# Cross-attention on one core: idle matrix products in TensorE's start, newer landing times in the plan, and other orders of the units of work

## The chip, the cores and the metric

The kernel runs on one core of one Trainium2 chip. The metric is the device time of one execution in microseconds (us): the median of 3 runs was 1946.18 us (1946.05 to 1948.58). Five engines work side by side, each through its own list of instructions in order: TensorE (PE, with its weight loads as PEld), VectorE (DVE), ScalarE (ACT), GpSimd (POOL) and SyncE (SP, which here only issues transfers).

## The reference

x and y (`ctx_2048`) are 32 x 256 x 1024, float32; the weights are 256 x 256.

```python
x_q = jnp.einsum('oc,bcn->bno', w_qk, y)
x_k = jnp.einsum('oc,bcn->bon', w_qk, x)
x_v = jnp.einsum('oc,bcn->bon', w_v, x) + b_v[None, :, None]
energy = jnp.einsum('bnc,bcm->bnm', x_q, x_k)
attention = jax.nn.softmax(energy, axis=-1)
attention = attention / (1e-07 + attention.sum(axis=1, keepdims=True))
x_r = jnp.einsum('bcn,bnm->bcm', x_v, attention)
x_r = jax.nn.relu(jnp.einsum('oc,bcn->bon', w_t, x - x_r) + b_t[None, :, None])
return x + x_r
```

## The kernel before

**The work.** Each of the 32 batches is a list of units. Every full-size number is split into three parts (tiles with a form index HIGH, LOW, REST), and each product is made as three products of parts, so one unit is 12 products of 128 x 512 on TensorE. The units of a batch, by the letters that the program uses:

- `k0`, `k1` (keys): x times the squared weight `gw`, into `gf`. ACT and DVE turn the sums into three forms.
- `v0`, `v1` or `V0`, `V1` (values): x times `vw`. DVE transposes the result into `turned`; SP writes `turned` to DRAM (`blocks`, four transfers) and reads it back in another layout (into `yr` or `turned`); ACT and POOL make the three forms `uf`.
- `W0`, `W1`: x times `tw`, which ACT copies to `xe` with a bias.
- `E0` to `E7` (energies): a 128 x 1024 tile of `energy`, from `gf` and the forms `yf` of y. DVE takes its minimum (`small<-banks`), ACT the exponential with a sum (`banks<-banks,small`), DVE the reciprocal; then for each half DVE adds to `acc`, ACT writes the HIGH form (`ef<-banks,small`), DVE the REST form (`ef<-banks,small,ef`), and last ACT and POOL the LOW form.
- `A0` to `A7`: `uf` times `ef`, summed over the eight tiles.
- `S`, `O`: sums of `acc`, and the end of a batch on DVE, POOL and ACT (`z`), with its stores.
- `X`, `Y2`, `Y3`: loading and splitting of the next x and y. y's forms are made with transfers that add, issued by POOL (`yf<-in_ctx_dram`, `yf<-yf`).

A batch has 22 units in the steady order: 8 E, 8 A, 2 k, 2 v, 2 W.

**Banks.** PSUM's eight banks are four pairs. The pairs of banks (4,5) and (6,7) hold the sums of the A units from A0 to A7, and outside that time other units, marked `^` in the orders; unmarked units take the pairs (0,1) and (2,3) in turn. A unit can start only when the pair that it takes has been read for the last time.

**What sets the order.** Five strings (`SET_UP`, `FIRST` for batch 0, `STEADY` for batches 1 to 29, `BEFORE` for batch 30, `LAST` for batch 31) give the order of the units on TensorE. The class `Plan` takes every instruction with an estimated duration, an estimated time from issue to landing, and what it reads and writes; it gives each a due time and sets the orders of the other engines from those. What it decides is then fixed: each engine takes its instructions in that order, so an instruction that waits holds up all behind it on its engine.

**Set-up.** `idle` products of the zero tile `few` (5 of them) come first on TensorE, then the square of w_qk (`G`, `banks<-z`), then the first keys (`f` with form, channel block and half), between them the transposes of w_t (`T`), the product of the bias (`b`) and the product of w_v and w_t (`Q`), all on raw x, w and y as they land.

**The end.** In the last batch `D1`, `G0` and `F1` finish the two halves of the channels: `F1` adds W1 straight into the sums of A, in pieces of 512, 256 and 256 columns.

All instructions carry line 231 of the profile, a helper that keeps each engine in order, so that they are told apart by their tiles.

Of the kernel before, what the change touches and what calls it, by code (L numbers as in the profile page):

```python
# [16 lines left out]
class Plan:  # L17
# [147 lines left out]


SET_UP = (
    "x0 x1 G fH00 fH10 fR10 fR00 T fH01 y fL01 fH11 b fR11 fR01 Q fL00 fL11 fL10"
)
FIRST = (  # L170
    "V0^ W1^ E0^ E1 V1^ W0^ E2 X E3 A0 A1 E4 E5 A2 A3 E6 E7 Y2 A4 A5 Y3 k1 v0 A6 A7 k0 S O"
)
STEADY = (
    "W0 E0^ E1 E2 V1^ W1^ E3 Y2 X A0 E4 A1 E5 A2 E6 A3 E7 A4 k1 A5 Y3 A6 v0 A7 S k0 O"
)
BEFORE = (
    "V1 E0^ E1 W0^ W1^ E2 A0 E3 E4 A1 A2 Y2 E5 E6 A3 E7 S A4 X Y3 A5 v0 A6 k1 k0 A7 O"
)
LAST = (
    "E0 R E1^ V1^ E2 E3 A0 A1 E4 A2 E5 A3 E6 E7 A4 A5 W0 A6 S a0 a1 D1 F1 G0"  # L180
)


# [1 line left out]
def kernel(  # L185
# [74 lines left out]
    def by_sync(landing, reads, writes, trace, early=0.0):  # L260
        plan.add("sync", 0.4, landing, reads, writes, trace, early=early)
# [13 lines left out]
    def accumulate(into, from_):  # L275
        pool.dma_start(into, from_, accum_op=ALU.add)
# [50 lines left out]
    def load_y(q):  # L327
        b, half = divmod(q, MH)
        s = q % NY
        f, r = yf[s], yr  # L330
        from_ = y[b].rearrange("(k p) n -> p k n", p=P)[:, :, ts(half, MB)]
        by_sync(7.0 if q else 7.8, [], ["yr"], lambda: sync.dma_start(r, from_))
        on_act(N, ["yr"], y_names(s, HIGH), lambda: act.copy(f[:, HIGH], r))

        def pieces(which):
            at = slice(which[0] * QB, (which[-1] + 1) * QB)
            high, low, third = (f[:, j, :, at] for j in range(FORMS))
            nh, nl, nr = (y_names(s, j, which) for j in range(FORMS))
# [12 lines left out]
            by_pool(8.0, nl + nr, nl, lambda: accumulate(value(low), value(third)))  # L351

        for which in ([0], [1]) if q == 0 else ([0, 1],):
            pieces(which)
# [4 lines left out]
    def load_x(b):  # L359
        for k in range(KC):  # L360

            def of(k=k):
                raw = [f"xr{k}{h}" for h in range(MH)]
                by_sync(6.0, [], raw, lambda: sync.dma_start(xr[:, k], x[b, ts(k, P)]))
                on_act(N, raw, x_names(HIGH, k), lambda: act.copy(xf[:, HIGH, k], xr[:, k]))
                on_pool(
                    N, raw + x_names(HIGH, k), x_names(REST, k),
# [4 lines left out]
                    lambda: act.mul(xf[:, LOW, k], value(xf[:, HIGH, k]), 1.0 / UP),  # L372
                )
                by_pool(
                    9.0, x_names(LOW, k) + x_names(REST, k), x_names(LOW, k),
                    lambda: accumulate(value(xf[:, LOW, k]), value(xf[:, REST, k])),
                )

# [41 lines left out]
    def values(b, q, j_pair):  # L420
# [151 lines left out]
    def finish(b):  # L572
        for c in range(KC):

            def of(c=c):
# [10 lines left out]
                by_sync(6.0, ["bias"], ["xo"], lambda: sync.dma_start(xo, x[b, ts(c, P)]))  # L586
# [5 lines left out]

            of()

    def ready_end(b):

        c = KC - 1
        raw = [f"xr{c}{h}" for h in range(MH)]
        on_act(
            N, raw + ["bias"], raw,  # L600
            lambda: act.activation(xr[:, c], xr[:, c], AF.Identity, bias=xbias[:, c], scale=1.0),
        )
# [35 lines left out]

            of()

    def end(b, c):

        p = pair(2 + c)
        for h in range(MH):
            cuts = [(0, MB)] if (c, h) != (KC - 1, MH - 1) else [(0, MB // 2), (MB // 2, MB)]
            for lo, hi in cuts:
                for j in ORDER:

# [197 lines left out]
    def set_up(token):  # L846
# [25 lines left out]
    def do(b, token):  # L872
# [15 lines left out]
        elif kind == "O":  # L888
            finish(b)
        elif kind == "R":  # L890
            ready_end(b)
        elif kind == "D":
            divided(n)
        elif kind == "G":
            beside(b, n)
        elif kind == "F":
            end(b, n)
        elif kind == "Y":
            if 2 * b + n < MH * B:
                load_y(2 * b + n)  # L900
# [45 lines left out]
```

## Time and profile before

| | |
|---|---|
| median of 3 runs | 1946.18 us (1946.05 to 1948.58) |
| the profiled execution, its own time | 1945.59 us |
| its span, first to last instruction | 1943.6 us |
| mean granted TensorE clock over the span | 0.998 |
| DMA, mean | 155 GB/s |

A time in the timeline is counted from the start of the span. A row gives start, duration (of a merged group: from its first start to its last end), engine, line, operation, tiles written and read, and count; in square brackets stands how long the engine sat idle before it, and what ended that. A row of the table by stage gives for each stretch the busy time of each engine with its count, the granted clock of TensorE (1.00 is full speed), the share of the DMA engines and GB/s.

### The profile page before, as it was taken

The page shows a single profiled execution, that of the slowest core. Times are in us where ns is not written, and L with a number is a line of the kernel's source. Part 1 is how long each engine was busy: PE and PEld are TensorE (multiplying, and loading weights), DVE is VectorE, ACT ScalarE, POOL GpSimd, SP SyncE. Part 2 cuts the span into 40 slices and gives each one's busy share as a digit, 9 for nine tenths or more (in the row PEclk, how much of TensorE's full clock was granted, in tenths as well). Part 3 has the DMA queues.
Part 4 walks back from the last instruction along what each step waited for, and adds up shares of the span by engine and source line. Part 5 has one row for each costly group of instructions (what it writes and reads, how often), then busy time and mean ns, then how long its engine had stood idle before and what let it go on. Part 6 is the DMA issues. An engine that isn't in the chain of part 4 may idle for free.

```text
span 1943.6 us, 24348 instructions
## 1 busy us (share of the span) xinstructions
PE 1930.7 (99%) x8492; PEld 1594.9 (82%) x8492; DVE 1496.1 (77%) x2107; ACT 1470.7 (76%) x1929; POOL 1554.5 (80%) x775
## 2 busy tenths in 40 slices
PE   9999999999999999999999999999999999999998
PEld 7788888888888888888888888888888888888877
DVE  6787777777777877778777777777787777877777
ACT  6679777797777887777977779777788777787665
POOL 5789777888777887778977788877888777897766
PEclk9999999999999999999999999999999999999999
DMA  6666765766666666666676576756666666667542
GB/s 178 142 155 166 178 151 132 163 167 177 155 141 148 163 174 174 141 149 157 164 181 149 132 163 167 179 155 139 151 163 174 171 142 147 158 165 182 141 98 76
DMA packets 128779, 301.75 MB, mean 155 GB/s; under 512 B 12944, under 2 KB 47248, under 8 KB 128656
## 3 DMA queue, kind: packets, MB, share of 16 engines
q1 hardware_dynamic: 92256, 200.19, 33.5%
q0 software_dynamic: 35680, 99.10, 29.7%
q8 instruction: 66, 1.08, 0.2%
q10 hardware_dynamic: 720, 0.92, 0.2%
q14 instruction: 57, 0.47, 0.1%
HBM read 167.25 MB, written 67.11 MB: 121 GB/s over the span
## 4 chain that ended last, share of the span: by engine, by line
PE 96%; DMA 1%; DVE 1%; ACT 0%; SPq 0%; POOL 0%; issue 0%; DVEq 0%
PE banks L231 96%; DMA blocks<-turned 1%; DMA yr<-blocks 1%; SPq L231 0%; POOL uf L231 0%; DVE ef L231 0%; DVE z L231 0%; DVE turned L231 0%; DVE acc L231 0%; DVE small L231 0%; POOL z L231 0%; ACT banks L231 0%; ACT uf L231 0%; ACT z L231 0%; ACT xe L231 0%
## 5 line engine op out<-in xcount | busy, mean ns | idle before, releaser
L231 PE MATMUL banks<-gf,yf 128*128 128x512 f32 x3072 | 730.2, 390 | 4.8 <-DVE ef L231 4.1
L231 POOL TENSOR_TENSOR ef<-ef 128x1024 fp32r<-128x1024 f32 x256 | 643.3, 2515 | 114.5 <-ACT ef L231 84.4
L231 PE MATMUL banks<-ef,uf 128*128 128x512 f32 x3072 | 731.7, 389 | 0.0
L231 PEld LDWEIGHTS banks<-gf,yf 128*128 128x128 f32 x3072 | 576.9, 188 | 127.6 <-DVE ef L231 6.6
L231 PEld LDWEIGHTS banks<-ef,uf 128*128 128x128 f32 x3072 | 577.0, 188 | 119.7
L231 DVE TENSOR_REDUCE small<-banks 128x1 f32<-128x1024 f32 x256 | 313.1, 1223 | 128.9 <-PE banks L231 126.6
L231 DVE SCALAR_TENSOR_TENSOR ef<-banks,small,ef 128x512 fp32r<-128x512 f32 x512 | 363.2, 741 | 21.6 <-ACT ef L231 21.4
L231 ACT ACTIVATE ef<-banks,small 128x512 fp32r<-128x512 f32 x512 | 333.9, 701 | 17.5 <-DVE acc L231 9.7
L231 ACT ACTIVATE gf<-banks 128x1024 fp32r<-128x1024 f32 x64 | 65.7, 1028 | 341.2 <-PE banks L231 341.0
L231 DVE SCALAR_TENSOR_TENSOR acc<-banks,small,acc 128x512 f32<-128x512 f32 x448 | 316.1, 746 | 6.8
L231 ACT ACTIVATE banks<-banks,small 128x1024 f32<-128x1024 f32 x256 | 280.6, 1096 | 38.4 <-DVE small L231 35.0
L231 ACT ACTIVATE ef<-ef 128x1024 fp32r<-128x1024 f32 x256 | 274.7, 1073 | 2.1
L231 POOL TENSOR_TENSOR z<-z,xe 128x1024 f32<-128x1024 f32 (+1 forms) x64 | 150.3, 2364 | 107.9 <-DVE z L231 105.4
L231 POOL TENSOR_TENSOR uf<-yr,uf 128x1024 fp32r<-128x1024 f32 x64 | 153.4, 2397 | 70.3 <-ACT uf L231 70.3
L231 PE MATMUL banks<-xf,gw 128*128 128x512 f32 x768 | 186.5, 392 | 1.9 <-ACT xf L231 1.9
L231 PE MATMUL banks<-xf,tw 128*128 128x512 f32 (+1 forms) x774 | 185.2, 388 | 1.6 <-DVE ef L231 0.7
L231 PE MATMUL banks<-xf,vw 128*128 128x512 f32 x768 | 184.6, 389 | 0.0
L231 POOL TENSOR_TENSOR uf<-turned,uf 128x1024 fp32r<-128x1024 f32 x64 | 167.6, 2619 | 5.7 <-DVE acc L231 3.3
L231 PEld LDWEIGHTS banks<-xf,tw 128*128 128x128 f32 x774 | 144.4, 188 | 32.8 <-DVE ef L231 1.7
L231 PEld LDWEIGHTS banks<-xf,gw 128*128 128x128 f32 x768 | 144.6, 189 | 32.5 <-ACT xf L231 2.3
L231 DVE RECIPROCAL small<-small 128x1 f32<-128x1 f32 x256 | 40.4, 158 | 168.5 <-ACT banks L231 168.5
L231 PEld LDWEIGHTS banks<-xf,vw 128*128 128x128 f32 x768 | 144.1, 188 | 30.2 <-DVE vw L231 0.3
(69 smaller groups left out, 1704.4 us busy)
## 6 DMA issues: line engine op xcount, KB each, us to landing
yr<-in_ctx_dram SPq DMA_DIRECT2D x64, 512.0 KB, 4.9
blocks<-turned SPq DMA_DIRECT2D x256, 128.0 KB, 2.9
yf<-in_ctx_dram POOLq DMA_DIRECT2D x63, 512.0 KB, 6.4
yf<-yf POOLq DMA_DIRECT2D x63, 512.0 KB, 4.7
xr<-in_x_dram SPq DMA_DIRECT2D x62, 512.0 KB, 4.2
xo<-in_x_dram SPq DMA_DIRECT2D x62, 512.0 KB, 4.5
xf<-xf POOLq DMA_DIRECT2D x62, 512.0 KB, 7.6
out_dram<-z SPq DMA_DIRECT2D x62, 512.0 KB, 4.9
```

The lines of the kernel that those rows point to most:

```text
L231: self.last = getattr(self.engine, name)(*args, **kwargs)
```

## The change

It does four things.

1. A token `z` in `SET_UP` issues one idle product of the zero tile `few` on TensorE. There is one before `G` and three behind it, beside the five that were there. The set-up's tokens also stand in another order: among others, the first key products are those of x's second channel block (`fH10`), and the load of y (`y`, which is enqueued on SP) stands behind `fH10`.
2. The estimated landing times in the plan are changed (y 7.0 to 5.8, x 6.0 to 5.0, the adding transfers 9.0 and 8.0 to 7.2 and 5.8, x's 9.0 to 8.2, `blocks` 2.4 to 3.0 and back 3.2 to 4.5, xo 6.0 to 5.2), and the estimated duration of the idle products and squares. These are inputs of the planner; no transfer is changed.
3. All five orders of the units are replaced. Of this table the diff shows two lines.
4. `R` takes its channel from the token and `end` is told whether it is the last; with the tokens `R1` and `F1` they issue what they issued before.

Apart from the four idle products no instruction is added or removed; the rest are moved.

```diff
 SET_UP = (
-    "x0 x1 G fH00 fH10 fR10 fR00 T fH01 y fL01 fH11 b fR11 fR01 Q fL00 fL11 fL10"
+    "x1 z G z z x0 z fH10 y fH00 fR10 T fH01 fL10 b fR01 fR00 fL01 Q fL00 fH11 fL11 fR11"
 )
...
 STEADY = (
-    "W0 E0^ E1 E2 V1^ W1^ E3 Y2 X A0 E4 A1 E5 A2 E6 A3 E7 A4 k1 A5 Y3 A6 v0 A7 S k0 O"
+    "W0^ E0^ E1 E2 W1^ V1^ E3 Y2 A0 E4 A1 E5 A2 X E6 A3 E7 Y3 S A4 A5 v0 k1 A6 A7 k0 O"
 )
...
-        by_sync(7.0 if q else 7.8, [], ["yr"], lambda: sync.dma_start(r, from_))
+        by_sync(5.8 if q else 7.8, [], ["yr"], lambda: sync.dma_start(r, from_))
...
-            by_pool(9.0, nr, nr, lambda: accumulate(third, from_[:, :, at]))
+            by_pool(7.2, nr, nr, lambda: accumulate(third, from_[:, :, at]))
...
-        plan.add("sync", 2.4, 2.4, ["turned"], ["blocks"], out_of)
+        plan.add("sync", 2.4, 3.0, ["turned"], ["blocks"], out_of)
         back, name = (turned, "turned") if q else (flat(yr), "yr")
-        by_sync(3.2, ["blocks"], [name], lambda: sync.dma_start(back, blocks))
+        by_sync(4.5, ["blocks"], [name], lambda: sync.dma_start(back, blocks))
...
-        plan.add("pe", count * (columns * 4 / 2400 - 0.08), 0.163, reads, writes, trace)
+        plan.add("pe", count * columns * 3.4 / 2400, 0.163, reads, writes, trace)
 
-    fp32_on_pe(
-        5, P, ["few"], ["bank7"],
-        lambda: [pe.matmul(banks[:, 7, :P], few, few, start=True, stop=True) for _ in range(5)],
-    )
+    def idle_products(count):
+        fp32_on_pe(
+            count, P, ["few"], ["bank7"],
+            lambda: [pe.matmul(banks[:, 7, :P], few, few, start=True, stop=True) for _ in range(count)],
+        )
+
+    idle_products(5)
...
+        elif token == "z":
+            idle_products(1)
```

**TensorE, the first rows of the program.** `few` is the tile of zeros, `z` holds the raw weights, `xf` the forms of x, `gw` those of the squared weight. Before:

```order
L231 MATMUL banks_95<-few_66 128x128 x5
L231 MATMUL banks_95<-z_90 128x256 x4
L231 MATMUL banks_95<-xf_74,gw_71 128x512 x8
L231 MATMUL banks_95<-z_90 128x128 x4
L231 MATMUL banks_95<-xf_74,gw_71 128x512 x6
```

The same place now:

```order
L231 MATMUL banks_95<-few_66 128x128 x6
L231 MATMUL banks_95<-z_90 128x256 x4
L231 MATMUL banks_95<-few_66 128x128 x3
L231 MATMUL banks_95<-xf_74,gw_71 128x512 x6
L231 MATMUL banks_95<-z_90 128x128 x4
```

One idle product stands ahead of the square and three between it and the first keys; the transposes come after 6 key products, where it was 8.

**TensorE, from A5 of batch 0 to the first energies of batch 1.** `uf1` and `ef` belong to the A units, `vw` to the values v0, `gw` to the keys k0 and k1, `tw` to W0, `yf0` to E0, E1 and E2. Before:

```order
L231 MATMUL banks_95<-ef1_81,uf1_77 128x512 x12
L231 MATMUL banks_95<-xf_74,gw_71 128x512 x12
L231 MATMUL banks_95<-xf_74,vw_72 128x512 x12
L231 MATMUL banks_95<-ef2_82,uf1_77 128x512 x12
L231 MATMUL banks_95<-ef3_83,uf1_77 128x512 x12
L231 MATMUL banks_95<-xf_74,gw_71 128x512 x12
L231 MATMUL banks_95<-xf_74,tw_73 128x512 x12
L231 MATMUL banks_95<-gf_75,yf0_78 128x512 x36
```

The same place now:

```order
L231 MATMUL banks_95<-ef1_81,uf1_77 128x512 x12
L231 MATMUL banks_95<-xf_74,vw_72 128x512 x12
L231 MATMUL banks_95<-ef2_82,uf1_77 128x512 x12
L231 MATMUL banks_95<-xf_74,gw_71 128x512 x12
L231 MATMUL banks_95<-ef3_83,uf1_77 128x512 x12
L231 MATMUL banks_95<-xf_74,gw_71 128x512 x12
L231 MATMUL banks_95<-xf_74,tw_73 128x512 x12
L231 MATMUL banks_95<-gf_75,yf0_78 128x512 x36
```

The values v0 stand one unit earlier: five units lie between them and E0 of the next batch, where there were four.

**ACT, in the last batch, from the keys' HIGH forms to the first energies.** `gf` are the keys, `uf0` the forms of v0, `banks,small` the exponentials (of E0, then of E1), `z` the end of batch 30, `ef0` the forms of E0. Before:

```order
L231 ACTIVATE gf_75<-banks_95 128x1024 x2
L231 CAST uf0_76<-yr_85 128x4x4x64
L231 ACTIVATE uf0_76<-uf0_76 128x1024
L231 ACTIVATE banks_95,small_93<-banks_95,small_93 128x1024
L231 ACTIVATE z_90<-z_90 128x1024
L231 ACTIVATE banks_95,small_93<-banks_95,small_93 128x1024
L231 ACTIVATE ef0_80<-banks_95,small_93 128x512 x2
L231 ACTIVATE ef0_80<-ef0_80 128x1024
```

The same place now:

```order
L231 ACTIVATE gf_75<-banks_95 128x1024 x2
L231 CAST uf0_76<-yr_85 128x4x4x64
L231 ACTIVATE banks_95,small_93<-banks_95,small_93 128x1024
L231 ACTIVATE z_90<-z_90 128x1024
L231 ACTIVATE banks_95,small_93<-banks_95,small_93 128x1024
L231 ACTIVATE ef0_80<-banks_95,small_93 128x512 x2
L231 ACTIVATE uf0_76<-uf0_76 128x1024
L231 ACTIVATE ef0_80<-ef0_80 128x1024
```

The second step on `uf0`, which needs POOL's work on the first, has moved from ahead of the exponential of E0 to behind the HIGH forms of E0.

More of the change, by code (lines that the diff above doesn't have):

```diff
@@ L363, in of @@
                 raw = [f"xr{k}{h}" for h in range(MH)]
-                by_sync(6.0, [], raw, lambda: sync.dma_start(xr[:, k], x[b, ts(k, P)]))
+                by_sync(5.0, [], raw, lambda: sync.dma_start(xr[:, k], x[b, ts(k, P)]))
                 on_act(N, raw, x_names(HIGH, k), lambda: act.copy(xf[:, HIGH, k], xr[:, k]))
@@ L374, in of @@
                 by_pool(
-                    9.0, x_names(LOW, k) + x_names(REST, k), x_names(LOW, k),
+                    8.2, x_names(LOW, k) + x_names(REST, k), x_names(LOW, k),
                     lambda: accumulate(value(xf[:, LOW, k]), value(xf[:, REST, k])),
@@ L585, in of @@
                 on_act(N, [f"z{c}"], [f"z{c}"], lambda: act.activation(z[:, c], z[:, c], AF.Relu))
-                by_sync(6.0, ["bias"], ["xo"], lambda: sync.dma_start(xo, x[b, ts(c, P)]))
+                by_sync(5.2, ["bias"], ["xo"], lambda: sync.dma_start(xo, x[b, ts(c, P)]))
                 on_pool(
@@ L593, in finish, with ready_end @@
             of()
-    def ready_end(b):
-        c = KC - 1
+    def ready_end(c):
         raw = [f"xr{c}{h}" for h in range(MH)]
@@ L639, in beside, with end @@
             of()
-    def end(b, c):
+    def end(b, c, last):
         p = pair(2 + c)
         for h in range(MH):
-            cuts = [(0, MB)] if (c, h) != (KC - 1, MH - 1) else [(0, MB // 2), (MB // 2, MB)]
+            cuts = [(0, MB)] if not last or h != MH - 1 else [(0, MB // 2), (MB // 2, MB)]
             for lo, hi in cuts:
@@ L890, in do @@
         elif kind == "R":
-            ready_end(b)
+            ready_end(n)
         elif kind == "D":
@@ L896, in do @@
         elif kind == "F":
-            end(b, n)
+            end(b, n, token == [t for t in LAST.split() if t[0] == "F"][-1])
         elif kind == "Y":
```

8 lines of the change are left out of this document (4 added, 4 removed).

## Prediction

> **What bounds the kernel now.** I read the page, the chain of work in order of time, TensorE's waits, and TensorE's timeline, in that order. The page's first part:
>
> ```profile
> span 1943.6 us, 24348 instructions
> ...
> PE 1930.7 (99%) x8492; PEld 1594.9 (82%) x8492; DVE 1496.1 (77%) x2107; ACT 1470.7 (76%) x1929; POOL 1554.5 (80%) x775
> ```
>
> TensorE is the bound: it idles for 12.9 us of the span, and no product is removed. The chain shows how much of that lies in the steady batches:
>
> ```profile
> 100.12 1763.28 PE banks L231 x7776
> ```
>
> 7776 products in 1763.28 us are 0.2268 us each, 2.721 us for a unit of twelve. From here to 1863 the chain never leaves TensorE. So an order of units can win nothing in the steady batches, only lose there; what can be won lies before 100 and behind 1863. TensorE's longest waits:
>
> ```profile
> PE banks L231 <- DVE ef L231: 4.8, 3, 2.6
> PE banks L231 <- ACT xf L231: 1.9, 1, 1.9
> ...
> PE banks L231 <- ACT xe L231: 0.7, 1, 0.7
> ```
>
> Its timeline shows where (start, duration, operation; in brackets the idle time before):
>
> ```profile
> 8.53 3.15 PE L231 MATMUL banks<-xf,gw 128*128 128x512 f32 x8 [1.89 <-ACT xf L231]
> ...
> 18.92 3.02 PE L231 MATMUL banks<-xf,vw 128*128 128x512 f32 x12
> ...
> 40.45 3.06 PE L231 MATMUL banks<-gf,yf 128*128 128x512 f32 x12 [1.45 <-DVE ef L231]
> 43.35 5.60 PE L231 MATMUL banks<-ef,uf 128*128 128x512 f32 x24
> ...
> 73.74 2.88 PE L231 MATMUL banks<-xf,vw 128*128 128x512 f32 x12
> ...
> 87.34 5.60 PE L231 MATMUL banks<-gf,yf 128*128 128x512 f32 x24
> ...
> 105.93 2.88 PE L231 MATMUL banks<-ef,uf 128*128 128x512 f32 x12
> ```
>
> and at the end
>
> ```profile
> 1882.27 5.60 PE L231 MATMUL banks<-gf,yf 128*128 128x512 f32 x24
> ...
> 1890.43 2.88 PE L231 MATMUL banks<-gf,yf 128*128 128x512 f32 x12
> 1895.94 4.61 PE L231 MATMUL banks<-gf,yf 128*128 128x512 f32 x12 [2.63 <-DVE ef L231]
> 1900.38 5.60 PE L231 MATMUL banks<-ef,uf 128*128 128x512 f32 x24
> ...
> 1936.11 2.36 PE L231 MATMUL banks<-xf,tw 128*128 128x512 f32 x12 [0.17 <-DVE banks L231]
> ```
>
> Counting units between these starts gives the loss of each stretch against 2.721 us a unit. V0 to A0 of batch 0 (18.92 to 43.35, 8 units): 24.43 - 21.77 = 2.7. A0 to E0 of batch 1 (16 units): 43.99 - 43.54 = 0.5. E0 to A0 of batch 1 (6 units): 18.59 - 16.33 = 2.3. From there to E2 of the last batch (656 units) nothing. E2 to A0 of the last batch (2 units): 9.95 - 5.44 = 4.5. A0 to the last product group (13 units): 35.73 - 35.37 = 0.4. Beside that stands the set-up, where TensorE's clock matters too:
>
> ```profile
> 9.00:10.00 1.00, 1.00 (x5) 0.64 (x4) 1.00 (x1) 0.00 (x0) 1.00 (x2) 0.68 0.71 208
> 10.00:11.00 1.00, 1.00 (x3) 0.76 (x3) 1.00 (x2) 0.00 (x0) 0.92 (x2) 0.50 0.15 15
> 11.00:12.00 1.00, 1.00 (x5) 0.74 (x4) 0.97 (x2) 0.00 (x0) 1.00 (x1) 0.50 0.00 0
> 12.00:13.00 1.00, 1.00 (x5) 0.81 (x4) 1.00 (x2) 0.43 (x1) 0.25 (x1) 0.61 0.76 209
> ...
> 40.00:60.00 20.00, 19.55 (x84) 15.61 (x84) 14.65 (x23) 19.91 (x28) 19.78 (x10) 1.00 0.69 185
> ...
> 1897.00:1898.00 1.00, 1.00 (x4) 0.81 (x3) 1.00 (x3) 0.37 (x2) 1.00 (x1) 0.50 0.98 261
> ```
>
> The last three numbers of a row are clock, DMA share and GB/s. Right behind the wait of 1.89 us the clock is halved for 0.32 + 0.50 + 0.50 + 0.39 = 1.71 us of lost work, and again behind the wait of 2.63 us: there twelve products take 4.61 us where the group before took 2.88, so 1.73 of the 4.5 us are the clock. The wait of 1.45 us in batch 0 left it at 1.00.
>
> **The change part by part.** Set-up. One more idle product ahead of the square and three behind it. Two rows price them:
>
> ```profile
> 1.05 2.50 PE L231 MATMUL banks<-few 128*128 128x128 f32 x10 [1.05 <-DVE parts L231]
> 3.40 3.23 PE L231 MATMUL banks<-z 128*128 128x256 f32 x8
> ```
>
> Five products (ten records) fill 1.05 to 3.40, 0.47 each. The first added one delays the square by up to 0.47 us, and with it the weights' forms on ACT and DVE; the first key product would then start near 9.0 instead of 8.53. Against that it is now a product of x's second block, whose HIGH form DVE makes, not ACT's last step: I take 8.6. The three behind the square end between 7.8 (0.24 each at full clock) and 8.5, so of the idle 1.89 us at most 0.8 stay. That is shorter than waits after which the clock held, so I take the 1.71 us as saved and charge 0.2 for the later square: -1.5 us for the start of V0. The bounds: +0.3 (clock still halved, square later) and -2.4 (part of the gap goes too).
>
> The Trainium skill's page "TensorE: Matmul & The Clock Gate" (Part 1: The HAM clock gate) says the clock is halved after an idle window of about 3.4 us and comes back after a busy one of that length. The length agrees with the 3.4 us at half speed here; that an idle stretch must be that long doesn't, since 1.89 and 2.63 us were enough, and the measurement decides. By the page the idle products would save no clock at all.
>
> SP's queue there: y's load now stands behind the two small bias loads. ACT's first use of y comes behind the copy of w_t, so some 2 us of delay are covered; if they aren't, ACT's steps for `vw` wait behind it and V0 with them.
>
> Batch 0 up to A0. Four rows of ACT and POOL show what the losses hang on (the cast that starts v0's or V0's forms waits for the transfer back):
>
> ```profile
> 34.40 1.05 ACT L231 CAST uf<-yr 128x1024 fp32r<-128x1024 f32 x1 [1.84 <-DMA yr<-blocks]
> ...
> 91.54 1.05 ACT L231 CAST uf<-yr 128x1024 fp32r<-128x1024 f32 x1 [4.75 <-DMA yr<-blocks]
> ...
> 1885.68 1.05 ACT L231 CAST uf<-yr 128x1024 fp32r<-128x1024 f32 x1 [4.91 <-DMA yr<-blocks]
> 1889.24 1.06 ACT L231 ACTIVATE uf<-uf 128x1024 fp32r<-128x1024 f32 x1 [2.51 <-POOL uf L231]
> 1890.21 1.07 ACT L231 ACTIVATE banks<-banks,small 128x1024 f32<-128x1024 f32 x1
> ```
>
> and the page prices the softmax steps (mean ns behind the comma):
>
> ```profile
> L231 DVE TENSOR_REDUCE small<-banks 128x1 f32<-128x1024 f32 x256 | 313.1, 1223 | 128.9 <-PE banks L231 126.6
> L231 DVE SCALAR_TENSOR_TENSOR ef<-banks,small,ef 128x512 fp32r<-128x512 f32 x512 | 363.2, 741 | 21.6 <-ACT ef L231 21.4
> L231 ACT ACTIVATE ef<-banks,small 128x512 fp32r<-128x512 f32 x512 | 333.9, 701 | 17.5 <-DVE acc L231 9.7
> ...
> L231 ACT ACTIVATE banks<-banks,small 128x1024 f32<-128x1024 f32 x256 | 280.6, 1096 | 38.4 <-DVE small L231 35.0
> ```
>
> The cast lands 15.5 us after V0's start (34.40 - 18.92). Now E0's HIGH forms stand behind it on ACT, and E2 takes E0's banks: 15.5 + 1.05 + 0.70 + 0.74 = 18.0, against 6 units = 16.3. So a wait of 1.7 us moves from E3 to E2; E2 and E3 then run through, and A0 comes at 18.0 + 5.4 = 23.4 instead of 24.4: -1.0 us. Bounds 0 (something new at E3) and -2.6 (an earlier landing).
>
> Turn to batch 1. v0 ends at 73.74 + 2.88 = 76.6, its data are back at 91.5, 14.9 us later. ACT's exponential of E0 stands behind that cast. Before, E0 ended 5 units (13.6 us) after v0, and cast, `xe` and `z` (about 1.05 each) took the exponential to 14.9 + 3.2 = 18.1, where DVE's minimum had it ready at 13.6 + 1.4 = 15.0. Now E0 ends 6 units (16.3 us) after v0, its minimum at 17.7, and `xe` and `z` stand ahead of the cast: 14.9 + 1.05 = 16.0 is in time by 1.7. I take all of it: -2.2 us; bounds -1.0 and -2.3.
>
> Last batch. The distance from v0 to E0 is four units as before, so I let the cast start 3.4 us after E0's start again (1885.68 - 1882.27); the collision with y's adding transfers, which can't start until E7 is done, stays. What goes is the step `uf<-uf` with its 2.51 us of waiting for POOL, ahead of the exponential. That was at 1890.21, 7.9 us after E0's start; now 3.4 + 1.05 = 4.5. Then exponential 1.10, `z` 1.05 (like the cast), E1's exponential 1.10, HIGH 0.70, two RESTs 0.74 each: 9.9. E3 needs the first half at 4 units = 10.9. So it doesn't wait, and without the wait the clock isn't halved: -4.4 us of the 4.5. What is late next is A0's LOW form on POOL, by my sum just in time. Bounds -2.0 and -4.5.
>
> The end. `G0` and `F1` change places on DVE, which reads a 256-column piece before the 512-column one; TensorE's wait for that stays, and the last store may go up to 0.3 us later: +0.2.
>
> Steady batches, 29 of them. Units are only reordered, so the price is 0 as long as no step comes too late. Two places are tight. W0^ now takes the pair (6,7), which the end of the batch before still reads:
>
> ```profile
> 1041.36 2.48 DVE L231 SCALAR_TENSOR_TENSOR z<-banks,ubias,rc 128x1024 f32<-128x1024 f32 x2 [0.96 <-PE banks L231]
> ```
>
> (DVE; one such step has a mean of 1279 ns:)
>
> ```profile
> L231 DVE SCALAR_TENSOR_TENSOR z<-banks,ubias,rc 128x1024 f32<-128x1024 f32 x62 | 76.7, 1279 | 28.6 <-PE banks L231 28.6
> ```
>
> and on TensorE W0 of the next batch:
>
> ```profile
> 1044.33 2.88 PE L231 MATMUL banks<-xf,tw 128*128 128x512 f32 x12
> ```
>
> DVE is through at 1043.84, W0 starts at 1044.33: 0.5 us in hand. And V1^ takes E0's pair. Counted from W0^'s start, E1 ends at 8.16; min of E1 to 9.4, its exponential to 10.5, E0's HIGH to 11.2, REST 11.9, `acc` (taken as a REST) 12.7, min of E2 13.9, second REST 14.6. V1^ reaches that bank at 13.60 + 1.36 = 14.96: 0.3 us in hand. v0 stands two units earlier against k0, which gives its transfers 5.4 us more. I take 0; bounds 0 and +0.7 a batch, one DVE step of 0.74.
>
> The landing times in the plan issue nothing. The sum: -1.5 - 1.0 - 2.2 - 4.4 + 0.2 = -8.9 us. The profiled execution took 1945.59 us, 0.6 below the median of 1946.18; 1945.59 - 8.9 = 1936.7, as a median **1937.3 us**. By the bounds the forecast's own range is 1934.4 to 1942.2. A measurement of this kernel can tell about 0.2% (3.9 us) from no change.
>
> **The rivals.** (a) Slower: V1^ waits in each steady batch. The place is the bank of E0's second REST; it decides when that step is 0.3 us later than my sum, and outweighs the gain from 0.31 us a batch (8.9 / 29) beyond that. With one DVE step more in the way the wait is 0.74 - 0.3 = 0.44, or 12.8 us: 1950. For it: the small margin, and an in-order ACT and DVE. Against: the two `z` steps above take 2.48 us together at 1.279 each, so steps in a row overlap a little and my sum is on the late side. 0.11. (b) The gain is eaten up: a steady wait of about 0.2 us (5.8 us), or the transfer in the last batch lands later, E3 waits as before and the clock falls again (4.4 us): 1942 to 1946, within 0.2%. For it: the losses hang on transfers that collide. 0.13. (c) Mending the gaps brings the gaps alone: no clock is saved in either place, 2 x 1.7 us less gain, 1940.7. For it: other idle stretches, not these, could set the clock. Against: each stretch at half speed follows such a wait. 0.06. The Trainium skill's page named above, by its idle window of 3.4 us, would have it so; it also calls that window free-running, so that the stretch could move from run to run, which no run here shows. The forecast has 0.70.
>
> **The numbers.** Faster by over 0.2% are the forecast and (c), 0.76; within it (b), 0.13; slower (a), 0.11. The range leaves out (a) and about half of (b), 0.17: 1934.5 to 1943.0.
>
> **What would show it.** Right: no halved clock near 10 or 1897; V0 near 17.4; a wait of 1 to 2 us ahead of E2 in batch 0, none near 93 to 100; E2 to A0 of the last batch in about 5.5 us; a chain that stays on TensorE from about 100 on at 0.2268 us a product. Wrong: a wait of TensorE that returns some 29 times, at V1^, W0^ or E3; a halved clock; ACT's cast of `uf` more than 4 us after E0's start in the last batch.

## The result, and the profile after

The changed kernel takes 1937.15 us (median of 5 runs, 1936.26 to 1939.32), against 1946.4 us (1946.05 to 1949.93) for the kernel before beside it: a ratio of 0.9948, 95% interval 0.9933 to 0.9962. The forecast was 1937.3. The profiled execution took 1936.26 us. The first lines of its page, and TensorE's waits (total, times, longest):

```profile
span 1934.5 us, 24348 instructions
...
PE 1926.5 (100%) x8500; PEld 1593.5 (82%) x8500; DVE 1493.8 (77%) x2107; ACT 1474.2 (76%) x1929; POOL 1549.4 (80%) x775
```

```profile
PE banks L231 <- DVE xf L231: 1.7, 3, 1.0
PE banks L231 <- DVE few L231: 1.1, 1, 1.1
...
```

TensorE idles for 8.0 us instead of 12.9; its waits for `ef` and `xe` are gone. The chain stays on it from batch 0 until 9 us before the end (start, duration, products):

```profile
35.26 1890.36 PE banks L231 x8337
```

That is 0.2267 us a product. TensorE's timeline, at the places that the prediction showed of before:

```profile
3.77 2.06 PE L231 MATMUL banks<-z 128*128 128x256 f32 x8
...
7.53 2.02 PE L231 MATMUL banks<-xf,gw 128*128 128x512 f32 x6 [1.02 <-DVE xf L231]
...
18.38 2.88 PE L231 MATMUL banks<-xf,vw 128*128 128x512 f32 x12
...
35.26 5.74 PE L231 MATMUL banks<-gf,yf 128*128 128x512 f32 x24
40.83 5.60 PE L231 MATMUL banks<-ef,uf 128*128 128x512 f32 x24
...
84.35 8.32 PE L231 MATMUL banks<-gf,yf 128*128 128x512 f32 x36
...
95.23 3.02 PE L231 MATMUL banks<-xf,vw 128*128 128x512 f32 x12
...
100.83 2.88 PE L231 MATMUL banks<-ef,uf 128*128 128x512 f32 x12
...
1877.03 5.60 PE L231 MATMUL banks<-gf,yf 128*128 128x512 f32 x24
...
1885.29 5.60 PE L231 MATMUL banks<-gf,yf 128*128 128x512 f32 x24
1890.73 5.61 PE L231 MATMUL banks<-ef,uf 128*128 128x512 f32 x24
...
1926.46 2.36 PE L231 MATMUL banks<-xf,tw 128*128 128x512 f32 x12 [0.17 <-DVE banks L231]
```

E2 and E3 of the last batch run through (1885.29, 24 products in 5.60 us), where a wait of 2.63 us and a group of 4.61 us stood. Read as stretches between the same units:

| stretch | before, us | after, us | change | forecast |
|---|---|---|---|---|
| span's start to V0 of batch 0 | 18.92 | 18.38 | -0.5 | -1.5 |
| V0 to A0 of batch 0 | 24.43 | 22.45 | -2.0 | -1.0 |
| A0 of batch 0 to E0 of batch 1 | 43.99 | 43.52 | -0.5 | 0 |
| E0 to A0 of batch 1 | 18.59 | 16.48 | -2.1 | -2.2 |
| A0 of batch 1 to E2 of the last batch | 1784.50 | 1784.46 | 0 | 0 |
| E2 to A0 of the last batch | 9.95 | 5.44 | -4.5 | -4.4 |
| A0 to the last product group (`F1`) | 35.73 | 35.73 | 0 | 0 |
| `F1` to the span's end | 7.49 | 8.04 | +0.6 | +0.2 |

ACT's rows of the last batch show the step that the forecast rested on: the cast lands 3.41 us after E0's start (1880.44 - 1877.03), as assumed, and the exponential of E0 stands right behind it.

```profile
1880.44 1.05 ACT L231 CAST uf<-yr 128x1024 fp32r<-128x1024 f32 x1 [4.89 <-DMA yr<-blocks]
1881.39 1.08 ACT L231 ACTIVATE banks<-banks,small 128x1024 f32<-128x1024 f32 x1
```

### The profile page after: what moved, and what is told of

Same layout as the page of the kernel before. It is cut to its first block, busy times and chain, and to the rows that moved or that the text cites. A ratio compares the mean times of both kernels' runs of the same rounds, so it can differ in the third digit from the quotient of the medians.

```text
span 1934.5 us, 24348 instructions
## 1 busy us (share of the span) xinstructions
PE 1926.5 (100%) x8500; PEld 1593.5 (82%) x8500; DVE 1493.8 (77%) x2107; ACT 1474.2 (76%) x1929; POOL 1549.4 (80%) x775
## 4 chain that ended last, share of the span: by engine, by line
PE 99%; DVE 1%; issue 0%; DVEq 0%; ACT 0%
PE banks L231 99%; DVE xf L231 0%; DVE z L231 0%; DVE banks L231 0%; DVE gw L231 0%; DVE xe L231 0%; DVEq L945 0%; ACT gw L231 0%; DVE few L231 0%; DVE nbias L231 0%; DVE ubias L231 0%
## 5 line engine op out<-in xcount | busy, mean ns | idle before, releaser
L231 POOL TENSOR_TENSOR ef<-ef 128x1024 fp32r<-128x1024 f32 x256 | 619.5, 2421 | 140.4 <-DVE acc L231 59.4
L231 DVE SCALAR_TENSOR_TENSOR ef<-banks,small,ef 128x512 fp32r<-128x512 f32 x512 | 369.9, 743 | 59.1 <-ACT ef L231 56.9
L231 POOL TENSOR_TENSOR xf<-xr,xf 128x1024 fp32r<-128x1024 f32 (+1 forms) x64 | 151.0, 2382 | 6.2 <-DVE xf L231 6.2
L231 POOL TENSOR_TENSOR uf<-turned,uf 128x1024 fp32r<-128x1024 f32 x64 | 155.2, 2424 | 0.0
```

The lines of the kernel that those rows point to most:

```text
L231: self.last = getattr(self.engine, name)(*args, **kwargs)
```

## The experiments

The theory at the start: the gains come from the mended waits, and the clock follows the waits. The rivals: the order of the units gives the gain and the numbers in the plan are idle, or the numbers give it; and the clock falls for another reason. Ratios are to the kernel before.

**1. The landing times alone, and the orders alone.** Two kernels, each with half of the change:

```diff
 landing_alone: the kernel before, with
-        plan.add("sync", 2.4, 2.4, ["turned"], ["blocks"], out_of)
+        plan.add("sync", 2.4, 3.0, ["turned"], ["blocks"], out_of)
...
 orders_alone: the changed kernel, with
-        by_sync(4.5, ["blocks"], [name], lambda: sync.dma_start(back, blocks))
+        by_sync(3.2, ["blocks"], [name], lambda: sync.dma_start(back, blocks))
...
```

> The five orders of the units and the set-up as before; only the landing times in the plan are the new ones. In the last batch the plan then puts ACT's step uf<-uf behind the exponential of E0, where it stood ahead of it. Theory (the landing times set ACT's order, and that order made the wait of the last batch): E2 to A0 of the last batch takes 5.4 to 5.6 us instead of 9.95, with no halved clock there, and the time is 4.4 us less than before, about 1942 us, if no new wait comes in the other batches. Rival (the orders of the units made the gain): E2 to A0 stays near 9.95 us and the time within 1 us of 1946.4. The set-up keeps its halved clock near 10 us by both, V0 at 18.9.

Measured: 1941.11 us (1939.51 to 1943.07), ratio 0.9971 (0.9961 to 0.9981). TensorE in the last batch:

```profile
1890.94 4.24 PE L231 MATMUL banks<-gf,yf 128*128 128x512 f32 x18
1895.38 1.67 PE L231 MATMUL banks<-gf,yf 128*128 128x512 f32 x6 [0.20 <-DVE ef L231]
1896.89 5.63 PE L231 MATMUL banks<-ef,uf 128*128 128x512 f32 x24
```

E2 to A0 takes 5.95 us: 4.0 of the 4.5 us come with the numbers alone, with every unit where it was. They are not all due to ACT's order: the transfer back also lands sooner there, and the cast starts 1.94 us after E0 (1884.62 - 1882.68), not 3.41. Batch 0 gains 1.2 us (V0 to A0 23.27), A0 to E0 of batch 1 the same 0.5 as in the changed kernel (43.52), the turn to batch 1 nothing (18.72).

> The changed kernel with the landing times of before in the plan; its unit orders, its four idle products and its durations on TensorE are kept, so TensorE's list is that of the changed kernel. In the last batch the plan puts ACT's uf<-uf ahead of the exponential of E0 again. Theory: the wait of 2.6 us ahead of E3 and the stretch at half speed come back, E2 to A0 near 9.9 us instead of 5.4, and the time is 4.4 us above the changed kernel, about 1941.5. Rival (the orders of the units made the gain): 1937, with E2 to A0 near 5.4. Batch 0 and the turn to batch 1 keep their gain (V0 to A0 near 22.5 us, E0 to A0 of batch 1 near 16.5) if the unit orders made it there.

Measured: 2002.95 us (1998.44 to 2005.63), ratio 1.0289 (1.0274 to 1.0303). Both forecasts of the time fell. E2 to A0 of the last batch took 6.46 us, with the cast 1.5 us after E0's start. Batch 0 keeps its gain (V0 to A0 21.76 us), the turn to batch 1 doesn't (18.21). The traced execution takes 62.2 us more than that of the changed kernel: 49.7 of it lie in the steady batches, in rival (a) of the prediction, 3.0 ahead of them and 9.5 behind. TensorE's waits, then ACT, DVE and TensorE in one steady batch, whose W0 starts at 1132.16:

```profile
PE banks L231 <- DVE ef L231: 40.3, 32, 2.5
```

```profile
1136.55 1.05 ACT L231 CAST uf<-yr 128x1024 fp32r<-128x1024 f32 x1 [3.15 <-DMA yr<-blocks]
...
1140.41 1.04 ACT L231 ACTIVATE uf<-uf 128x1024 fp32r<-128x1024 f32 x1
1141.35 1.07 ACT L231 ACTIVATE banks<-banks,small 128x1024 f32<-128x1024 f32 x1
...
1143.89 1.09 ACT L231 ACTIVATE banks<-banks,small 128x1024 f32<-128x1024 f32 x1 [1.35 <-DVE small L231]
```

```profile
1142.65 1.20 DVE L231 TENSOR_REDUCE small<-banks 128x1 f32<-128x1024 f32 x1
...
1145.09 1.21 DVE L231 TENSOR_REDUCE small<-banks 128x1 f32<-128x1024 f32 x1
1146.22 0.74 DVE L231 SCALAR_TENSOR_TENSOR ef<-banks,small,ef 128x512 fp32r<-128x512 f32 x1
```

```profile
1147.02 3.06 PE L231 MATMUL banks<-xf,vw 128*128 128x512 f32 x12 [1.09 <-DVE ef L231]
```

V1 waits for E0's banks in nearly every batch. The exponential of E0 starts 9.2 us after W0, behind `uf<-uf`. DVE takes E1's minimum (1142.65) only behind the reciprocal of E0, in the changed kernel ahead of it; ACT waits 1.35 us for that ahead of E1's exponential, and E0's HIGH forms stand behind both. Last, the minimum of E2 (1145.09) stands ahead of E0's first REST step. W0 of batch 1 to W0 of batch 29 is 1725.42 us here and 1675.68 in the changed kernel: 1.78 us a batch over 28. So the new orders need the new numbers: without them they are 3% slower than the kernel before.

**2. Which numbers.** Two of the landing times belong to the transfer out and back (`blocks` and back); one kernel has only those old, one has only those new, both with the new orders.

```diff
 back_old: the changed kernel, with blocks 2.4 and back 3.2
 back_only: the changed kernel, with y 7.0, 9.0 and 8.0, x 6.0 and 9.0, xo 6.0
```

> The changed kernel with two numbers of the plan as before: blocks 2.4 instead of 3.0, and the transfer back 3.2 instead of 4.5; the other landing times are the new ones. The plan then has ACT's uf<-uf ahead of the exponential of E0 in 28 steady batches and in the last. Theory (these two numbers alone made the 66 us between the orders with old and with new landing times): V1 waits in nearly all steady batches, 1.2 to 1.7 us lost each, and the time is 1995 to 2008 us. Rival (the numbers of the adding transfers of x and y made it): at most 1942.

Measured: 1945.78 us (1943.95 to 1948.23), ratio 0.9998 (0.9989 to 1.0007).

> The changed kernel with only those two numbers new (blocks 3.0, back 4.5); the landing times of x, y, xo and of the adding transfers are those of before. ACT's uf<-uf then stands behind the exponential of E0 everywhere. Theory: within 2 us of the changed kernel, 1935 to 1939, no wait that returns in the steady batches, E2 to A0 of the last batch under 6 us. Rival (the other landing times are needed too): over 1945.

Measured: 1948.26 us (1943.66 to 1952.9), ratio 1.0008 (0.9998 to 1.0018). Both theories fell: neither group of numbers alone gives back the 66 us, and neither gives the 1937. From W0 of batch 1 to W0 of batch 29 `back_old` takes 1677.81 us and `back_only` 1681.97, so 2.1 and 6.3 more than the changed kernel; in `back_old` 1.8 of the 2.1 lie in batch 1, and the other batches lose next to nothing. (The runs of `back_only` spread over 9 us, and its trace is of one of 1945.01 us, among the shorter.) In a batch from the middle of `back_old` the cast comes 2.9 us after W0 instead of 4.4, so `uf<-uf` ahead of the exponential does no harm there; its own losses stand in the set-up (V0 at 21.88) and in the last batch (E2 to A0 7.66).

**3. One step moved.** So that nothing else moves, the next kernels change the lists after the planner is done: ACT's `uf<-uf` is put ahead of the exponential of E0, in the last batch, or in the 28 batches 2 to 29.

```diff
...
-        for op, _ in out:
+        for op in [o for op in out if op not in self.low + self.step for o in (*ahead.get(id(op), ()), op)]:
             op.trace()
...
```

> The changed kernel with one instruction of ACT moved: in the last batch the step uf<-uf stands ahead of the exponential of E0, as before the change; all other lists are the same. Theory (this place of one step made the wait of the last batch, and the wait made the stretch at half speed): the cast of uf starts 3.4 us after E0's start, uf<-uf waits 2.5 us for POOL, the exponential of E0 starts 7.9 us after E0's start instead of 4.4, TensorE waits about 2.6 us ahead of E3 and runs at 0.50 for 3.4 us behind it; E2 to A0 takes 9.9 us instead of 5.4, and the time is 4.5 us above the changed kernel, about 1941.6. Rival (the new order of the units leaves room for the step): E2 to A0 under 6 us and the time within 1 us of 1937.2.

Measured: 1938.24 us (1937.48 to 1940.05), ratio 0.9959 (0.9947 to 0.9972), E2 to A0 5.51 us. This doesn't count against the theory: ACT's step stood ahead of the POOL step whose result it scales, so it scaled what was in the tile before (the LOW form of the first half of the last batch's values is changed by this) and waited for nothing. The next run moves the POOL step too.

> The changed kernel with ACT's uf<-uf of the last batch, and the POOL step that it reads, put ahead of the exponential of E0; all other lists the same, and POOL's own order too. (In the run uf_first only ACT's step had been moved, so that it no longer waited for POOL.) Theory: the cast of uf starts 3.4 to 3.9 us after E0's start, uf<-uf waits 2.5 us for POOL, the exponential starts at 7.9 to 8.4, TensorE waits 2.6 us or more ahead of E3, over what halves the clock in the ladder of gaps (between 1.69 and 2.01 us), so E2 to A0 takes 9.9 to 10.5 us instead of 5.44 and the time is 4.5 to 5 us above the changed kernel, 1941.5 to 1942.5. Rival: E2 to A0 under 7 us, and 1938 or less.

Measured: 1941.78 us (1940.48 to 1943.09), ratio 0.9975 (0.9965 to 0.9984). The median is the one expected; the trace is so only in part. ACT, then TensorE:

```profile
1885.40 1.06 ACT L231 ACTIVATE uf<-uf 128x1024 fp32r<-128x1024 f32 x1 [2.61 <-POOL uf L231]
1886.37 1.07 ACT L231 ACTIVATE banks<-banks,small 128x1024 f32<-128x1024 f32 x1
```

```profile
1891.08 3.06 PE L231 MATMUL banks<-gf,yf 128*128 128x512 f32 x12 [1.63 <-DVE ef L231]
```

The exponential starts 8.1 us after E0 (1878.31), like the 7.9 before the change, but E3 waits for 1.63 us and not 2.63, and twelve products take 3.06 us, so the clock held. E2 to A0 is 7.73 us. DVE's rows of the kernel before hold the missing 1.0 us:

```profile
1894.00 1.25 DVE L231 STREAM_TRANSPOSE turned<-banks 128x1024 f32<-128x1024 f32 x1
1895.17 0.71 DVE L231 SCALAR_TENSOR_TENSOR ef<-banks,small,ef 128x512 fp32r<-128x512 f32 x1
```

There DVE turned V1 ahead of E0's REST step, for which E3 waited; in the changed kernel and in `uf_last` it stands behind it. That part was read from the traces and not tried by itself.

> The changed kernel with ACT's uf<-uf ahead of the exponential of E0 in the 28 batches 2 to 29; every other list as in the changed kernel. Theory (a late transfer back and uf<-uf ahead of the exponential make V1 wait together, each alone doesn't): the cast stays at 4.7 us after W0's start, uf<-uf then waits for POOL and the exponential starts about 9.2 us after W0's start instead of 7.6; V1 has 0.3 us in hand, so it waits 1.3 us in each of the 28 batches and loses 1.3 to 1.9 us there with what follows: 36 to 53 us, 1973 to 1990 us. Rival (the place of the step is harmless, and something else made the waits of the orders with the old landing times): within 5 us of 1937.

Measured: 1946.76 us (1946.06 to 1948.68), ratio 1.0007 (0.9998 to 1.0016): 9.6 us above the changed kernel, neither the 36 to 53 of the theory nor the rival's 5 at most. ACT and TensorE in a batch whose W0 starts at 1046.78:

```profile
1056.11 1.07 ACT L231 ACTIVATE banks<-banks,small 128x1024 f32<-128x1024 f32 x1
```

```profile
1062.34 1.65 PE L231 MATMUL banks<-xf,vw 128*128 128x512 f32 x6 [0.44 <-DVE ef L231]
```

The exponential is late as computed (9.3 us after W0 instead of 7.6), but E0's second REST step ends only 0.9 us later (15.5 us after W0 instead of 14.6), since DVE had waited in between; 0.3 of that was in hand. 0.32 us a batch are lost. So the place of `uf<-uf` is a sixth of the 1.78 us of `orders_alone`. The rest goes with DVE's order there. E0's exponential starts at nearly the same place in both (9.2 and 9.3 us after W0), but its HIGH forms start at 12.8 us in `orders_alone` and at 11.6 here, because of E1's late minimum; E2's minimum ahead of the first REST step adds to that, and the first half of V1 has to wait. That order was not tried alone, and which of the numbers of x, y and xo sets it stays open.

**4. The clock.** A ladder of gaps ahead of the changed kernel, with nothing else on DVE:

```diff
...
+    for copies in (1, 2, 3, 4, 5, 6, 7, 8, 9, 10, 12, 14, 3, 4, 5, 6, 7, 4, 5, 6):
+        gap(copies)
...
```

> The changed kernel with a ladder ahead of it: 21 blocks of 40 idle products of zeros (about 9.4 us each at full clock), between them 20 gaps in which TensorE waits for 1 to 14 small copies on DVE (some 0.3 to 4 us); it adds about 220 us, which mean nothing. Theory (a single idle stretch somewhere between 1.45 and 1.89 us is enough to halve the clock for 3.4 us): a gap up to 1.4 us is followed by 1.00, one of 1.9 us or more by 0.50 for about 3.4 us, each time. Rival (an idle stretch must last the full 3.4 us, and the stretches before were chance): only gaps over 3.4 us halve the clock. A third case (what counts is the idle share of a free-running window of 3.4 us): gaps between 1.4 and 2 us halve it in some cases and not in others.

Measured on TensorE (two records a product; 80 take 9.20 us at full clock):

```profile
1.05 12.68 PE L231 MATMUL banks<-few 128*128 128x128 f32 x90 [1.05 <-DVE parts L231]
...
55.70 9.20 PE L231 MATMUL banks<-few 128*128 128x128 f32 x80 [1.68 <-DVE rc L231]
66.91 10.82 PE L231 MATMUL banks<-few 128*128 128x128 f32 x80 [2.01 <-DVE rc L231]
...
185.38 9.20 PE L231 MATMUL banks<-few 128*128 128x128 f32 x80 [1.69 <-DVE rc L231]
```

All gaps up to 1.69 us cost nothing behind them; all from 2.01 to 3.31 cost 1.62 us (those of 3.96 and 4.61, 1.36 and 2.26). But the length of a wait isn't the whole rule. `orders_alone` has two waits of over 2.2 us that left the clock at full speed (twelve products in 3.0 us), between others that halved it (4.5 to 4.6 us):

```profile
960.62 4.60 PE L231 MATMUL banks<-xf,vw 128*128 128x512 f32 x12 [2.50 <-DVE ef L231]
...
1763.39 3.02 PE L231 MATMUL banks<-xf,vw 128*128 128x512 f32 x12 [2.29 <-DVE ef L231]
...
1826.00 3.01 PE L231 MATMUL banks<-xf,vw 128*128 128x512 f32 x12 [2.23 <-DVE ef L231]
...
1885.84 4.51 PE L231 MATMUL banks<-xf,tw 128*128 128x512 f32 x12 [2.19 <-DVE ef L231]
```

What parts them is when the clock can fall. The ladder's first five waits of over 2 us end 13.15, 13.49, 13.80 and 14.14 us apart, but the granted clock in the trace falls every 13.65 us behind them: four times 3.41 us, which is also how long a stretch at half speed lasts. The falls of `orders_alone` at 960.64 and 1885.65 us are 271 times 3.413 us apart. So the falls keep to a grid of 3.41 us that doesn't follow the waits.

If the time of each trace is cut into pieces by its grid, the idle time within one piece decides. In all the traces, up to 1.78 us in a piece left the clock up (that was the part of the 2.23 us; of the 2.29 us it was 1.68), and 1.84 us or more brought it down (an idle stretch of 1.84 us in `clock_kept`, below; 2.42 of the 2.63 us in the kernel before). One fall, at 15.15 us in the set-up of `orders_alone`, fits only if products of one column count as idle: 1.28 us of its piece were idle, and 0.55 went on such products. This is the third case of the expectation; the ladder's own waits don't tell it from the theory, since each wait of over 2 us had 2.0 us or more in one piece. The Trainium skill's page "TensorE: Matmul & The Clock Gate" (Part 1: The HAM clock gate) gives an idle window of about 3.4 us for it; here 1.84 us of idle time in a piece of that length were enough.

```diff
 clock_kept: the kernel before, with
...
-    "E0 R E1^ V1^ E2 E3 A0 A1 E4 A2 E5 A3 E6 E7 A4 A5 W0 A6 S a0 a1 D1 F1 G0"
+    "E0 R1 E1^ V1^ E2 q E3 A0 A1 E4 A2 E5 A3 E6 E7 A4 A5 W0 A6 S a0 a1 D1 F1 G0"
...
+                lambda: [pe.matmul(banks[:, 7, :P], few, few, start=True, stop=True) for _ in range(10)],
...
```

> The kernel before with ten idle products of zeros put between E2 and E3 of the last batch, where TensorE waits for 2.63 us; all else as before. Theory (the stretch at half speed behind the wait is caused by the idleness, not by the wait's cause): the wait shrinks to some 0.3 us, clock 1.00 behind it, E3 takes 2.9 to 3.0 us instead of 4.61, E2 to A0 8.2 us instead of 9.95, and the time is 1.7 us less, about 1944.3. Rival (the clock falls there for another reason, or idle products of zeros don't hold it): E2 to A0 stays at 9.9 us and 1946.

Measured: 1947.23 us (1945.52 to 1950.6), ratio 1.0006 (0.9997 to 1.0015), and no theory was put to the test: the bank of the idle products was still to be read by DVE's transposition, so that they waited themselves, for 1.84 us, and the clock fell behind that.

```profile
1895.37 3.47 PE L231 MATMUL banks<-few 128*128 128x128 f32 x20 [1.84 <-DVE turned L231]
1898.49 3.77 PE L231 MATMUL banks<-gf,yf 128*128 128x512 f32 x12
```

So what the clock is worth in the last batch was read from one trace (4.61 us for E3 instead of 2.88) and not tried by itself. The whole times don't show it: of the 27 executions of the kernel before that ran beside this one, four have a mean granted clock of 1.000, where one stretch at half speed (1.7 us lost) would leave 0.999. They took 1946.1 to 1947.7 us, and the 27 have a median of 1946.4. No trace of the four is kept, so why they gained nothing stays open.

**5. The set-up.** The changed kernel without its four idle products, and the kernel before with three:

```diff
 no_idle:
-    "x1 z G z z x0 z fH10 y fH00 fR10 T fH01 fL10 b fR01 fR00 fL01 Q fL00 fH11 fL11 fR11"
+    "x1 G x0 fH10 y fH00 fR10 T fH01 fL10 b fR01 fR00 fL01 Q fL00 fH11 fL11 fR11"
 before_idle: three products of few behind G
```

> The changed kernel without its four added idle products; every engine's list is otherwise the same, the new set-up order included. Theory (the idle products keep the clock up, but DVE's forms of x set most of the start of V0): the wait ahead of the first key products is again 1.7 us or longer, the clock is halved for 3.4 us behind it, and V0 starts 0.3 to 1.2 us later than 18.38, because of the 1.7 us lost some lie beside waits for DVE. Rival one (idle products don't matter for the clock): clock 1.00 throughout, V0 at 18.4 or earlier. Rival two (the whole stretch at half speed counts): V0 at 20.1.

Measured: 1937.85 us (1936.03 to 1938.66), ratio 0.9955 (0.9942 to 0.9969), which the interval can't tell from the changed kernel. TensorE:

```profile
3.77 3.78 PE L231 MATMUL banks<-z 128*128 128x256 f32 x8 [0.22 <-DMA z<-in_L_xattn_w_qk_dram]
9.24 2.02 PE L231 MATMUL banks<-xf,gw 128*128 128x512 f32 x6 [1.69 <-DVE xf L231]
```

The wait is 1.69 us and the granted clock 1.00: under the 1.78 us that left the clock up, so in this execution the new order of the set-up alone keeps the clock. V0 came at 20.12, but all of its delay lies in the square, which took 3.78 us instead of 2.06; from its end to V0 it is 12.57 us, with the products 12.55.

> The kernel before with three idle products between the square of w_qk and the first key products, all other lists unchanged. Theory (they fill part of the 1.89 us, the clock isn't halved, and the 1.7 us of lost work are gained): idle under 1.3 us there, clock 1.00 from 9 to 13 us, and from the end of the square to V0 10.6 us instead of 12.3; 1.7 us less, 1944.7. Rival (the clock stays up, but V0 hangs on DVE's and POOL's forms of x and of w): clock 1.00, end of the square to V0 11.5 to 12.4, and the time within 1 us of 1946.4. Second rival (idle products of zeros don't hold the clock): 0.50 again.

Measured: 1947.23 us (1944.64 to 1948.4), ratio 1.0003 (0.9994 to 1.0012). The clock is 1.00 from 6 to 15 us, and nothing is won: the first rival, with more loss than it had foreseen. TensorE, DVE and POOL, and last the same DVE step in the kernel before:

```profile
8.63 2.37 PE L231 MATMUL banks<-xf,gw 128*128 128x512 f32 x8 [1.22 <-ACT xf L231]
...
20.41 3.06 PE L231 MATMUL banks<-xf,vw 128*128 128x512 f32 x12 [0.51 <-DVE vw L231]
```

```profile
15.37 3.15 DVE L231 TENSOR_SCALAR xbias<-nbias 128x2 f32<-128x2 f32 x1
18.44 0.68 DVE L231 SCALAR_TENSOR_TENSOR xf<-xf 128x512 fp32r<-128x512 f32 x1
```

```profile
15.51 1.74 POOL L231 TENSOR_TENSOR xe<-acc,tw 128x512 f32<-128x512 f32 x1
16.74 1.74 POOL L231 TENSOR_TENSOR yf<-yf 128x512 fp32r<-128x512 f32 x1
```

```profile
15.25 0.24 DVE L231 TENSOR_SCALAR xbias<-nbias 128x2 f32<-128x2 f32 x1
```

TensorE is faster, ACT's forms come sooner, POOL's two steps start 0.9 us earlier than before (16.38), and DVE's step of two columns now falls on them: 3.15 us instead of 0.24, ending when POOL's second step does (18.5). The last form of x comes 3.0 us later (18.44, before 15.40). V0 starts 13.7 us after the square's end, before 12.3.

**6. The end.** DVE's piece of 512 columns and its store put ahead of the first piece of 256 again, after the planner is done:

```diff
...
-        for op, _ in out:
+        for op in [o for op in out for o in (self.moved[:2] if op is self.moved[2] else []) + [op]]:
             op.trace()
...
```

> The changed kernel with one step of DVE and its store put back at the end: the piece of 512 columns of F1 is read and stored ahead of the first piece of 256. All else is the same. Theory: from F1's start to the end of the span 7.5 us, as before the change, instead of 8.04; 0.5 us less, which a median can hardly show: about 1936.7. Rival (the store's own time ends the span in any case): 8.0 us again. Its set-up is the changed kernel's, so V0's start tells how far that moves from one execution to another: 18.4 to 20.1 us, with the square of w_qk at 2.1 to 3.8 us and the rest, from its end to V0, at 12.5 to 12.6.

Measured: 1937.25 us (1936.47 to 1939.97), ratio 0.9957 (0.9945 to 0.997). From `F1`'s start to the end of the span it is 8.09 us: the order of the pieces was not the cause. DVE's last step ends 4.47 us after `F1`'s start (4.53 in the changed kernel, 4.42 before), and the span ends 3.6 us behind that (3.5, before 3.1), with the last store and the closing of the program. The stores land 2.0 to 2.5 us after their issue here, 1.8 to 2.2 in the changed kernel and 1.9 to 2.1 before; why the end takes longer stays open.

No version tried is faster than the changed kernel by its median.

## Why the prediction was right, and where its steps were off

The total was right (1937.3 against 1937.15, inside 1934.5 to 1943.0), and so were the two largest terms. That the total came to within 0.2 us is luck: the set-up and batch 0 were off by +1.0 and -1.0 us, two more stretches by -0.5 and +0.4, and the first two move by more than that from one execution to another.

**Set-up: wrong.** The step that failed is "so I take the 1.71 us as saved". The clock was kept, but the start of V0 didn't hang on TensorE. Five executions have the set-up lists of the changed kernel word for word (the result's, `uf_first`, `uf_last`, `uf_steady`, `tail_mended`): V0 starts at 18.38, 19.43, 19.20, 19.75 and 19.10, always 12.55 to 12.58 us behind the end of the square, where two executions with the lists of before have 12.29 and 12.24. So the new set-up is 0.3 us slower in that stretch, and the square starts 0.2 to 0.4 later. The -0.5 of the table is the luck of one execution, whose square took 2.06 us; the five V0 have a mean of 19.17, against 18.92 before. `before_idle` shows where such a gain can go: to DVE's steps beside POOL's.

**Batch 0: right in its mechanism, with a size that moves.** I took the landing of before, 15.5 us after V0's start, and got a wait of 1.7 us ahead of E2. The cast lands 14.3 to 14.4 us after V0 in three of the five executions, and 16.0 in the other two; in those the wait is there:

```profile
37.95 5.76 PE L231 MATMUL banks<-gf,yf 128*128 128x512 f32 x24 [1.65 <-DVE ef L231]
```

(`uf_first`; 1.53 in `uf_steady`). V0 to A0 is then 24.1 and 24.0 us, else 22.3 to 22.5; 24.4 before. What makes the transfer land 1.7 us sooner or later, issued at the same 9.4 us after V0, stays open.

**A0 of batch 0 to E0 of batch 1: not foreseen.** 0.5 us, which `landing_alone` gives as well.

**Turn to batch 1: right**, -2.1 against -2.2. Neither half of the change brings it: E0 to A0 takes 18.72 us in `landing_alone` and 18.21 in `orders_alone`, where V1 waits 1.36 us, against 18.59 before and 16.48 after. The order of the units that the prediction argued for needs the new numbers too.

**Last batch: right in size, and the step that goes was named right, but not all of the cause.** I put it down to `uf<-uf`. `uf_last` shows that this step alone brings back a wait of 1.63 us; 1.0 more goes with DVE's transposition by the traces, and the half clock (1.73 us) came behind the whole wait because 2.42 of its 2.63 us fell in one piece of the grid. The prediction gave no reason why the step moved, and set the plan's numbers down as issuing nothing. They do issue nothing, and yet they moved it: it stands behind E0's first HIGH form in `landing_alone`, with the units of before, and ahead of E0's exponential in `orders_alone`, with the new ones.

**Steady batches: right.** The margin of V1 was computed as 0.3 us; DVE's REST step and V1 (whose second bank comes 1.36 us behind its start, at 1054.19) in a steady batch of the changed kernel:

```profile
1053.13 0.74 DVE L231 SCALAR_TENSOR_TENSOR ef<-banks,small,ef 128x512 fp32r<-128x512 f32 x1
```

```profile
1052.83 2.88 PE L231 MATMUL banks<-xf,vw 128*128 128x512 f32 x12
```

1054.19 - 1053.87 = 0.3. Rival (a) is real: it needs only the old numbers in the plan, and costs 49.7 us in the steady batches then, more than the 12.8 that I gave it. Rival (c) is wrong for the last batch by the two traces, and right for the set-up in its time though not in its reason.

**The end**: +0.6 against +0.2, and not by the cause that I named.

## What to carry to other kernels

Where a planner turns estimated durations into fixed orders, its numbers and the order written by hand are one change: each half alone gave 1941 and 2003 us, together 1937, so price them together and read the resulting lists of the engines that are waited for. A clock that is kept up pays only if TensorE is what the next unit waits for; look first at which engine's form comes last. Before a stretch is credited to a change, see how far it moves between executions with the same lists: here the set-up moved by 1.4 us and batch 0 by 1.7.

## What the runs showed of the hardware

- **TensorE's clock** falls on a grid of 3.41 us that doesn't follow the waits. Idle time of up to 1.78 us within one piece of the grid left it up, 1.84 us or more halved it; one fall in a set-up came at 1.28 us, or 1.83 with the products of one column. So waits of up to 1.69 us never cost clock here by themselves; those of 2.19 and 2.50 us did, and those of 2.23 and 2.29 us didn't.
- **At the start of the program** TensorE runs at half pace though the granted clock reads 1.00: the ladder's first 90 records take 12.68 us, 2.33 more than 90 of the later ones. How long varies: in lists that are the same up to there, the square took 2.06, 2.76, 2.88, 3.07 and 3.42 us, and the first entry of the clock in the trace, ahead of which the views read 1.00, stands at 4.12, 5.51, 5.77, 6.16 and 6.86 us. The Trainium skill's page "TensorE: Matmul & The Clock Gate" (Part 1: The HAM clock gate) says that the window runs freely and that the slow stretch at the start differs from run to run; the squares here agree, and so do the falls on a grid of their own.
- **A step of DVE on two columns** took 3.15 us while POOL worked on two steps of 512 columns (`before_idle`, one execution), and 0.24 us beside none.
